# A graph-attention layer whose softmax picks one neighbour: another order of work after the last block of rows is read

## The chip, the cores and the metric

The kernel runs on one core of a Trainium2 chip, in float32. The metric is the device time of one execution in microseconds (us), as the median of several runs: 233.98 us for the kernel before (3 runs, 233.89 to 234.09).

## The reference

Inputs are x (4096 x 512), a dense matrix adj (4096 x 4096) that is added to the attention scores, W (512 x 2048, four heads of 512 columns) and a (four heads, 1024 numbers each). Cut to what matters:

```python
ht  = (x @ W) split into 4 heads
e   = leaky_relu(src[:, :, None] + dst[:, None, :], 0.01) + adj      # src, dst: ht times the two halves of a
att = softmax(e, axis=-1)
y   = (att @ ht).mean(over heads)
out = layernorm(x + y)                                               # over the 512 columns, eps 1e-5
```

The entries of adj go up to 1e9, while the scores are small. So in nearly every row the softmax is 1 at the largest entry of adj's row and 0 elsewhere, and y is that one row of x times the mean of the four heads of W. The kernel computes this, and also proves for each row that the largest entry leads the second by more than the scores can make up (a bound from the norms of x, W and a). Rows without that proof go through a second, general program, which is in the kernel but isn't entered on these data.

## The kernel before, in words

**Blocks.** The 4096 rows are 32 blocks of 128, numbered 0 to 31. A loop over t reads block t of adj (2 MB) by SyncE's DMA queue, five blocks ahead. VectorE takes the maxima of segments of each row (L215; for block 31 of the whole row, L208) and finds the segment with the largest; GpSimd gathers that segment (`lead`) and, when VectorE has found the column in it (L273, L281), the row of x that it names (`y`, L253 or L258). TensorE transposes y (`turn`, L287, into `tp`), ScalarE copies the result to SBUF (`yt`, L289), and TensorE multiplies it by the mean of W's heads (`products`, L306, four matmuls to a block, into a PSUM tile `o`). Most blocks get x by one more matmul with the identity (`residual`, L299). Blocks 22 to 27 don't: ScalarE puts their products by in SBUF (`put_by`, L354), since x for them lands late, in a buffer that adj has left, and GpSimd adds it (`add_x`, L358). Block 28 gets its x from VectorE (`add_sums`, L361), and so does block 30; block 31 is computed in two halves of 256 columns, each in its own PSUM tile.

**Normalising.** There are two ways. ScalarE sums a block and its squares (`stats`, L367 and L369), GpSimd makes shift and factor of the sums (`late_factors`, L385 to L387, the root by a power), and ScalarE scales (`finish`, L392). Or VectorE takes mean and variance (`moments`, L412 and L416), ScalarE the root (L418), VectorE the reciprocal (`factor`, L421, and with shift=True also minus mean times factor, L423), and then VectorE (`normalise`, L428) or ScalarE (`finish`) scales.

**The proof.** ScalarE sums the squares of each block of x (`row_norm`, L351) into a column of xx and takes the root of all (L623). `bound` finds the largest of them over all rows: VectorE's maximum along the columns (xm, L499), TensorE's transposition (px, L501), VectorE's maximum of that (xg, L503), TensorE's spreading over 128 partitions (px again, L506), ScalarE's bound from it (lead_by, L508). `test` (L514 to L521) compares the leads with it on VectorE, `count` adds up the rows that pass with a matmul (L527), `report` writes what is missing (any_bad, L531), which each engine reads before it decides on the general program.

**What sets the order.** Nothing reorders the instructions: the program is written out by hand, each engine takes its own instructions in the order in which the code names them, and waits on semaphores for the others. After the loop stands a long list of calls, the drain, in which blocks 28 to 31 are finished, blocks 22 to 27 get their x and are normalised, and the proof is completed. NB is 32, Q 4, LATE 28, BEHIND 24 and PUT 22. Stores go through SyncE's queue, also in order: 0 to 19 early, then 20 to 23, 28 and 29, 24 and 25, 26 and 27, 30, 31.

Of the kernel before, what the change touches and what calls it, by code (L numbers as in the profile page):

```python
# [13 lines left out]
AF = mybir.ActivationFunctionType  # L14
# [59 lines left out]
def leading_rows(ctx, tc, x, adj, W, a, out, ident, leads, any_bad):  # L74
# [14 lines left out]
    Q = 4  # L89
# [202 lines left out]
    def turn(ib):  # L292
        yt_of[ib] = turned_rows(y_t.pop(ib))

    def residual(ib):
        start = ib not in o_ps
        if start:
            o_ps[ib] = psum.tile([P, D], F32, name="o")
        nc.tensor.matmul(o_ps[ib], ident, hold[:, ib, :], start=start, stop=False)  # L299
# [48 lines left out]
    def row_norm(ib):  # L348
        sq = rows.tile([P, D], F32, name="sq")
        x_of = late_x[0][:, ib - PUT, :] if PUT <= ib < LATE else hold[:, ib, :]  # L350
        nc.scalar.activation(sq, x_of, AF.Square, accum_out=xx[:, ib : ib + 1])  # L351
# [8 lines left out]
    def add_sums(ib, out):  # L360
        nc.vector.tensor_add(out, o_ps[ib], hold[:, ib, :])  # L361
        o_ps[ib] = out
# [21 lines left out]
    def late_factors(i):  # L384
        nc.gpsimd.tensor_scalar(sd[:, i], sd[:, i], 1.0 / D, EPS, op0=OP.mult, op1=OP.add)  # L385
        nc.gpsimd.tensor_tensor(sd[:, i], sd[:, i], power[:, : i.stop - i.start], op=OP.pow)
        nc.gpsimd.tensor_mul(nm[:, i], nm[:, i], sd[:, i])  # L387

    def finish(ib):
        i = slice(ib, ib + 1)  # L390
        o = hold[:, ib, :] if ib < BEHIND else o_ps.pop(ib)
        nc.scalar.activation(hold[:, ib, :], o, AF.Identity, bias=nm[:, i], scale=sd[:, i])  # L392

    def residual_in_halves(ib):
        o_ps[ib] = [psum.tile([P, D // 2], F32, name="o") for _ in range(2)]
        for k, o in enumerate(o_ps[ib]):
            nc.tensor.matmul(o, ident, hold[:, ib, ts(k, D // 2)], start=True, stop=False)
# [10 lines left out]
    def moments(ib):  # L408

        if ib < NB - 1:  # L410
            st = small.tile([P, nc.vector.BN_STATS_DIM], F32, name="st", bufs=2)
            nc.vector.bn_stats(st, o_ps[ib])  # L412
        else:
            st = halves_st
        mv = mean_var[ib] = small.tile([P, nc.vector.BN_AGGR_DIM], F32, name="mv", bufs=3)
        nc.vector.bn_aggr(mv, st)  # L416
        r = rt[ib] = sd[:, ib : ib + 1]
        nc.scalar.activation(r, mv[:, 1:2], AF.Sqrt, bias=eps)  # L418
# [8 lines left out]
    def normalise(ib, o, columns=slice(0, D)):  # L427
        nc.vector.tensor_scalar(  # L428
            hold[:, ib, columns], o, mean_var[ib][:, 0:1], rt[ib], op0=OP.subtract, op1=OP.mult
        )  # L430
# [64 lines left out]
    def bound(part):  # L495

        if part == 0:
            xm = once.tile([P, 1], F32, name="xm")
            nc.vector.tensor_reduce(xm, xx, axis=AX.X, op=OP.max)  # L499
            px = of_bound[0] = psum.tile([1, P], F32, name="px", bufs=1)  # L500
            nc.tensor.transpose(px, xm, ident)  # L501
        elif part == 1:
            nc.vector.tensor_reduce(xg, of_bound[0], axis=AX.X, op=OP.max)  # L503
        elif part == 2:
            pb = of_bound[2] = psum.tile([P, 1], F32, name="px", bufs=1)
            nc.tensor.matmul(pb, ones[0:1, :], xg, start=True, stop=True)  # L506
        else:
            nc.scalar.activation(lead_by, of_bound[2], AF.Identity, bias=floor, scale=vn)  # L508
# [39 lines left out]
    for t in range(NB):  # L548
# [39 lines left out]
            row_norm(LATE)  # L588
            row_norm(LATE + 1)
        if t == NB - 1:  # L590
            for late in (PUT, PUT + 1):
                row_norm(late)
            residual(LATE + 1)
        if ib >= 0:
            if ib in TABLED:
                spread(ib)
# [20 lines left out]
        for done in FINISHED.get(t, ()):  # L617
            finish(done)

    for ib in (BEHIND, LATE + 2, BEHIND + 2):  # L620
        row_norm(ib)
        row_norm(ib + 1)
    nc.scalar.activation(xx, xx, AF.Sqrt, scale=1.05 ** 2)  # L623
    for ib in range(0, BEHIND - Q, Q):
        store(nc.sync, ib, Q)
    add_x(PUT)
# [5 lines left out]
        add_x(ib)  # L632
    products(LATE, KB - 1, KB)
    turn(NB - 3)
    residual_in_halves(NB - 1)
    products(NB - 3, 0, 2)
    moments(PUT)
    moments(PUT + 1)
    bound(0)
    stats(BEHIND)  # L640
    add_sums(LATE, o_ps[LATE])
    products(NB - 3, 2, KB - 1)
    moments(LATE)
    factor(PUT)
    normalise(PUT, o_ps.pop(PUT))
    bound(1)
    bound(2)
    bound(3)
    factor(PUT + 1)
    normalise(PUT + 1, o_ps.pop(PUT + 1))  # L650
    store(nc.sync, BEHIND - Q, Q)
    factor(LATE)
    normalise(LATE, o_ps.pop(LATE))
    for ib in range(BEHIND, NB - 1):
        find_inner(ib)
    turn(NB - 2)
    products(NB - 3, KB - 1, KB)
    stats(BEHIND + 1)
    late_factors(slice(BEHIND, BEHIND + 2))
    moments(NB - 3)  # L660
    test()
    products(NB - 2, 0, KB - 1)
    pg = count()
    stats(BEHIND + 2)
    late_factors(slice(BEHIND + 2, BEHIND + 3))
    factor(NB - 3)
    normalise(NB - 3, o_ps.pop(NB - 3))
    report(pg)
    finish(BEHIND)
    turn(NB - 1)  # L670
    products(NB - 2, KB - 1, KB)
    moments(LATE - 1)
    factor(LATE - 1, shift=True)
    finish(BEHIND + 1)
    products_of_half(NB - 1, 0)
    products_of_half(NB - 1, 1)
    add_sums(NB - 2, hold[:, NB - 2, :])
    moments(NB - 2)
    finish(BEHIND + 2)
    stats_of_half(NB - 1, 0)  # L680
    factor(NB - 2)
    normalise(NB - 2, o_ps.pop(NB - 2))
# [194 lines left out]
```

## Time and profile before

| | |
|---|---|
| median of 3 runs | 233.98 us |
| the profiled execution | 233.94 us |
| its span, first to last instruction | 232.4 us |
| busy: TensorE, VectorE, ScalarE, GpSimd | 84%, 84%, 64%, 49% |
| mean DMA rate over the span | 413 GB/s |
| last block of adj in use by VectorE | from 203.18 us |
| drain, from there to the last instruction of compute (229.02 us) | 25.8 us |

In the profile PE is TensorE, PEld its weight loads, DVE VectorE, ACT ScalarE, POOL GpSimd and SP SyncE. A row of a timeline has the start in us from the span's start, the length in us, engine, line and operation, what it writes and reads with shapes, and how many instructions are merged (x4); in brackets stands for how long the engine was idle just before, and what ended that. A float32 matmul is two records. Rows overlap by up to 0.1 us, since an engine begins an instruction before the last one's end is recorded. The chain of waits goes back from the last instruction, at each step to what released it.

### The profile page before, as it was taken

What the parts mean: (1) busy time and instruction counts of PE and PEld (TensorE: products, weight loads), DVE (VectorE), ACT (ScalarE), POOL (GpSimd) and SP (SyncE); (2) the same over time, 40 slices, a digit from 0 to 9 for tenths busy, and PEclk for the clock granted to TensorE, in tenths of its full rate; (3) what the DMA queues carried; (4) which work ended last, traced back from release to release, by engine and by line L of the source; (5) the groups of instructions that cost most, each with busy time, mean ns of one, the idle gap of its engine ahead of it and who ended that gap; (6) DMA issues with size and microseconds to landing.
All of it is one profiled execution on the core that took longest, in us unless ns stands there. A gap on an engine that the chain in (4) does not pass through costs nothing.

```text
span 232.4 us, 2519 instructions
## 1 busy us (share of the span) xinstructions
PE 196.0 (84%) x610; PEld 94.6 (41%) x610; DVE 194.1 (84%) x301; ACT 149.3 (64%) x371; POOL 113.5 (49%) x254
## 2 busy tenths in 40 slices
PE   0068988879069999999999899999999999999890
PEld 0023443333034445444444444454544445444360
DVE  0447299849999999999699959989999999889982
ACT  3004113597145988899988778778888746959572
POOL 4020414523555556555635665556556675468330
PEclk9999999999758999999999999999999999999999
DMA  6999999999999999999999999999999999999984
GB/s 223 434 429 430 429 430 425 433 433 422 423 437 425 414 438 427 424 427 426 428 432 424 425 429 429 425 426 430 426 430 414 420 424 421 421 420 430 426 330 193
DMA packets 12227, 96.04 MB, mean 413 GB/s; under 512 B 2020, under 2 KB 2468, under 8 KB 6064
## 3 DMA queue, kind: packets, MB, share of 16 engines
q1 hardware_dynamic: 8640, 88.08, 89.7%
q0 software_dynamic: 3552, 7.73, 8.5%
q8 instruction: 6, 0.10, 0.2%
q14 instruction: 13, 0.11, 0.1%
q10 hardware_dynamic: 16, 0.02, 0.0%
HBM read 88.51 MB, written 8.39 MB: 417 GB/s over the span
## 4 chain that ended last, share of the span: by engine, by line
DMA 38%; PE 29%; DVE 25%; ACT 3%; issue 2%; POOL 1%; SPq 0%; DVEq 0%; POOLq 0%
DMA adj_t<-in_adj_dram 29%; DVE seg L215 19%; PE o L306 18%; DMA hold<-in_L_gnn_W_dram 5%; DMA y<-in_x_dram,col 4%; PE o L346 3%; PE tp L287 3%; PE o L299 2%; DVE at L227 2%; DVE top L225 2%; PE o L401 2%; ACT sq L351 1%; DVE hold L428 1%; DVE within L273 1%; ACT off L336 0%
## 5 line engine op out<-in xcount | busy, mean ns | idle before, releaser
L215 DVE TENSOR_REDUCE seg<-adj_t 128x128 f32<-128x2048 f32 (+4 forms) x54 | 138.8, 2588 | 25.5 <-DMA adj_t<-in_adj_dram 25.4
L306 PE MATMUL o<-w_sum,yt 128*128 128x512 f32 x248 | 113.5, 597 | 1.1 <-ACT yt L289 1.1
L306 PEld LDWEIGHTS o<-w_sum,yt 128*128 128x128 f32 x248 | 46.7, 192 | 49.7 <-issue 42.3
L233 POOL DMA_INDIRECT lead<-in_adj_dram,row x31 | 32.5, 1048 | 14.5 <-POOL row L229 14.5
L229 POOL TENSOR_TENSOR row<-at,first 128x1 uint32<-128x1 uint32 x31 | 5.8, 188 | 60.6 <-DVE at L227 45.9
L258 POOL DMA_INDIRECT y<-in_x_dram,col x27 | 29.1, 1078 | 12.1 <-POOL col L275 6.8
L287 PE MATMUL tp<-ident,y 128*128 128x128 f32 x128 | 22.8, 302 | 10.0 <-DMA y<-in_x_dram,col 10.0
L452 PE MATMUL o<-hold,ident 128*128 128x512 f32 x32 | 15.7, 649 | 15.0 <-DMA hold<-in_L_gnn_W_dram 15.0
L287 PEld LDWEIGHTS tp<-ident,y 128*128 128x128 f32 x128 | 18.3, 210 | 20.7 <-issue 14.0
L289 ACT COPY yt<-tp 128x512 f32<-128x512 f32 x33 | 18.9, 572 | 11.5 <-PE tp L287 11.5
L336 ACT ACTIVATE off<-px,minus 128x128 f32<-128x128 f32 x27 | 9.9, 366 | 24.3 <-PE px L334 22.7
L299 PE MATMUL o<-hold,ident 128*128 128x512 f32 x46 | 24.4, 614 | 0.0
L346 PE MATMUL o<-z,pick 128*128 128x512 bf16 x81 | 22.6, 389 | 1.7 <-ACT pick L338 1.7
L392 ACT ACTIVATE hold<-hold,nm,sd 128x512 f32<-128x512 f32 x26 | 20.5, 802 | 0.0
L453 ACT ACTIVATE w_sum<-o 128x512 f32<-128x512 f32 x4 | 2.4, 597 | 22.9 <-PE o L452 22.9
L375 ACT ACTIVATE sq<-hold,nm 128x512 f32<-128x512 f32 x22 | 15.9, 722 | 0.7
L248 ACT COPY y<-zero 128x512 f32<-128x512 f32 x27 | 16.3, 603 | 0.0
L351 ACT ACTIVATE sq<-hold 128x512 f32<-128x512 f32 x26 | 16.2, 624 | 0.0
L452 PEld LDWEIGHTS o<-hold,ident 128*128 128x128 f32 x32 | 6.5, 211 | 23.3 <-issue 21.4
L346 PEld LDWEIGHTS <-pick 128*128 128x128 bf16 x81 | 7.6, 100 | 20.5 <-issue 9.3
L373 ACT ACTIVATE hold<-o 128x512 f32<-128x512 f32 x22 | 13.1, 597 | 0.7
L225 DVE MAX8 top<-seg 128x8 f32<-128x256 f32 (+2 forms) x31 | 11.3, 366 | 1.1
(117 smaller groups left out, 197.9 us busy)
## 6 DMA issues: line engine op xcount, KB each, us to landing
adj_t<-in_adj_dram SPq DMA_DIRECT2D x28, 2048.0 KB, 30.6
adj_t<-in_adj_dram SPq DMA_DIRECT2D x8, 1024.0 KB, 28.2
out_dram<-hold SPq DMA_DIRECT2D x5, 1024.0 KB, 17.2
hold<-in_L_gnn_W_dram SPq DMA_DIRECT2D x2, 2048.0 KB, 12.3
hold<-in_x_dram SPq DMA_DIRECT2D x3, 1024.0 KB, 32.6
hold<-in_x_dram SPq DMA_DIRECT2D x1, 1792.0 KB
hold<-in_x_dram SPq DMA_DIRECT2D x3, 512.0 KB, 24.1
out_dram<-hold SPq DMA_DIRECT2D x3, 512.0 KB, 2.8
```

Source lines behind the costliest of these rows:

```text
L215: nc.vector.tensor_reduce(seg_of[ib][:, ts(k, N // e // n)], adj_t[ib][:, ts(k, N // n)].rearrange("p (s e) -> p s e", e=e), axis=AX.X, op ...
L233: nc.gpsimd.indirect_dma_start(out=lead, out_offset=None, in_=adj_segs[e], in_offset=bass.IndirectOffsetOnAxis(ap=row[:, :1], axis=0),)
L248: nc.scalar.copy(y, zero.to_broadcast([P, D]))
L258: nc.gpsimd.indirect_dma_start(out=y_t[ib], out_offset=None, in_=x, in_offset=bass.IndirectOffsetOnAxis(ap=col[:, :1], axis=0), bounds_che ...
L287: nc.tensor.transpose(tp[:, kb, :], y[:, ds(kb, P, KB)], ident)
L289: nc.scalar.copy(yt, tp)
L299: nc.tensor.matmul(o_ps[ib], ident, hold[:, ib, :], start=start, stop=False)
L306: nc.tensor.matmul(o_ps[ib], yt_of[ib][:, kb, :], w_sum[:, kb, :], start=(start and kb == 0), stop=(kb == KB - 1),)
L346: nc.tensor.matmul(o_ps[ib], pick, z[k], start=(start and k == 0), stop=False)
L351: nc.scalar.activation(sq, x_of, AF.Square, accum_out=xx[:, ib : ib + 1])
L392: nc.scalar.activation(hold[:, ib, :], o, AF.Identity, bias=nm[:, i], scale=sd[:, i])
L452: nc.tensor.matmul(o, ident, hold[:, w_at + kb * H + h, :], start=(h == 0), stop=(h == H - 1))
```

## The change

All of it lies in the last pass of the loop and in the drain. The matmul that added x to block 29 is gone, and VectorE adds it after the products (L361, into PSUM). Blocks 22 and 23, which VectorE normalised, are scaled by ScalarE; VectorE computes their shift for it. The sum of squares of block 23 moves from the loop into the drain, and those of 26 and 27, with the root of all behind them, move behind the transposition of block 29. VectorE's maximum xm stands behind block 28's addition. The read of the largest norm (xg) stands ahead of VectorE's normalisations, its spreading behind the transposes of block 30. `test` stands ahead of block 29's addition and statistics. The sums of block 26 stand behind block 31's copy on ScalarE, and its factor comes from a root on ScalarE, a reciprocal and a product on VectorE (`last_factors`) in place of GpSimd's three instructions.

```diff
+    def last_factors(ib):
+        i = slice(ib, ib + 1)
+        nc.vector.reciprocal(sd[:, i], sd[:, i])
+        nc.vector.tensor_mul(nm[:, i], nm[:, i], sd[:, i])
@@ in the loop
         if t == NB - 1:
-            for late in (PUT, PUT + 1):
-                row_norm(late)
-            residual(LATE + 1)
+            row_norm(PUT)
@@ the drain
-    for ib in (BEHIND, LATE + 2, BEHIND + 2):
+    for ib in (PUT + 1, BEHIND, BEHIND + 1, NB - 2, NB - 1):
         row_norm(ib)
-        row_norm(ib + 1)
-    nc.scalar.activation(xx, xx, AF.Sqrt, scale=1.05 ** 2)
...
     turn(NB - 3)
+    row_norm(BEHIND + 2)
+    row_norm(BEHIND + 3)
+    nc.scalar.activation(xx, xx, AF.Sqrt, scale=1.05 ** 2)
     residual_in_halves(NB - 1)
     products(NB - 3, 0, 2)
     moments(PUT)
     moments(PUT + 1)
+    add_sums(LATE, o_ps[LATE])
     bound(0)
     stats(BEHIND)
-    add_sums(LATE, o_ps[LATE])
+    moments(LATE)
+    factor(PUT, shift=True)
+    factor(PUT + 1, shift=True)
     products(NB - 3, 2, KB - 1)
-    moments(LATE)
-    factor(PUT)
-    normalise(PUT, o_ps.pop(PUT))
     bound(1)
-    bound(2)
-    bound(3)
-    factor(PUT + 1)
-    normalise(PUT + 1, o_ps.pop(PUT + 1))
-    store(nc.sync, BEHIND - Q, Q)
     factor(LATE)
     normalise(LATE, o_ps.pop(LATE))
+    turn(NB - 2)
+    bound(2)
+    products(NB - 3, KB - 1, KB)
+    bound(3)
+    finish(PUT)
+    finish(PUT + 1)
+    store(nc.sync, BEHIND - Q, Q)
     for ib in range(BEHIND, NB - 1):
         find_inner(ib)
-    turn(NB - 2)
-    products(NB - 3, KB - 1, KB)
+    test()
     stats(BEHIND + 1)
     late_factors(slice(BEHIND, BEHIND + 2))
+    add_sums(NB - 3, o_ps[NB - 3])
     moments(NB - 3)
-    test()
     products(NB - 2, 0, KB - 1)
     pg = count()
+    report(pg)
+    turn(NB - 1)
+    products(NB - 2, KB - 1, KB)
     stats(BEHIND + 2)
-    late_factors(slice(BEHIND + 2, BEHIND + 3))
+    root(slice(BEHIND + 2, BEHIND + 3))
+    finish(BEHIND)
     factor(NB - 3)
     normalise(NB - 3, o_ps.pop(NB - 3))
-    report(pg)
-    finish(BEHIND)
-    turn(NB - 1)
-    products(NB - 2, KB - 1, KB)
     moments(LATE - 1)
-    factor(LATE - 1, shift=True)
     finish(BEHIND + 1)
     products_of_half(NB - 1, 0)
     products_of_half(NB - 1, 1)
+    last_factors(BEHIND + 2)
+    factor(LATE - 1, shift=True)
     add_sums(NB - 2, hold[:, NB - 2, :])
+    finish(BEHIND + 2)
     moments(NB - 2)
-    finish(BEHIND + 2)
```

The lines behind L388 move by five, so L428 before is L433 of the changed kernel. Three places of the engines' queues show what the diff does. VectorE around the read of the largest norm, before (from the addition of block 28; L428 are the normalisations of 22, 23 and 28):

```order
L361 TENSOR_TENSOR o<-o,hold 128x512
L412 BN_STATS st<-o 128x6
L416 BN_AGGR mv<-st 128x2
L421 RECIPROCAL sd<-sd 128x1
L428 TENSOR_SCALAR hold<-hold,mv,sd 128x512
L503 TENSOR_REDUCE xg<-px 1x1
L421 RECIPROCAL sd<-sd 128x1
L428 TENSOR_SCALAR hold<-hold,mv,sd 128x512
L421 RECIPROCAL sd<-sd 128x1
L428 TENSOR_SCALAR hold<-o,mv,sd 128x512
```

and in the changed kernel (L428 are now the shifts of 22 and 23, L433 the normalisation of 28):

```order
L361 TENSOR_TENSOR o<-o,hold 128x512
L504 TENSOR_REDUCE xm<-xx 128x1
L417 BN_STATS st<-o 128x6
L421 BN_AGGR mv<-st 128x2
L426 RECIPROCAL sd<-sd 128x1
L428 SCALAR_TENSOR_TENSOR nm<-mv,sd 128x1
L426 RECIPROCAL sd<-sd 128x1
L428 SCALAR_TENSOR_TENSOR nm<-mv,sd 128x1
L508 TENSOR_REDUCE xg<-px 1x1
L426 RECIPROCAL sd<-sd 128x1
L433 TENSOR_SCALAR hold<-o,mv,sd 128x512
```

The normalisations of 22 and 23 are gone from between the statistics of 28 and xg; a reciprocal and a shift of one column for each of the two blocks stand there.

TensorE in the same place, before (the two products are block 29's, then the transposition of xm, 29's third product, the spreading of xg, the transposes of block 30):

```order
L306 MATMUL o<-w_sum,yt 128x512 x2
L501 MATMUL px<-ident,xm 1x128
L306 MATMUL o<-w_sum,yt 128x512
L506 MATMUL px<-xg,ones 128x1
L287 MATMUL tp<-ident,y 128x128 x4
L306 MATMUL o<-w_sum,yt 128x512 x4
L527 MATMUL px<-leading,ones 1x1
```

and in the changed kernel:

```order
L306 MATMUL o<-w_sum,yt 128x512 x2
L506 MATMUL px<-ident,xm 1x128
L306 MATMUL o<-w_sum,yt 128x512
L287 MATMUL tp<-ident,y 128x128 x4
L511 MATMUL px<-xg,ones 128x1
L306 MATMUL o<-w_sum,yt 128x512 x4
L532 MATMUL px<-leading,ones 1x1
```

The transposes of block 30 now stand ahead of the matmul that spreads xg.

ScalarE towards the end, before (from block 25's sums; L418 are the roots of 29, 27, 30 and 31, L289 the copy of block 31, L392 the scaling of 24 to 27):

```order
L367 ACTIVATE sq,nm<-hold 128x512
L369 ACTIVATE sq,sd<-hold,nm 128x512
L418 ACTIVATE sd<-mv,eps 128x1
L367 ACTIVATE sq,nm<-hold 128x512
L369 ACTIVATE sq,sd<-hold,nm 128x512
L392 ACTIVATE hold<-hold,nm,sd 128x512
L289 COPY yt<-tp 128x512
L418 ACTIVATE sd<-mv,eps 128x1
L392 ACTIVATE hold<-hold,nm,sd 128x512
L418 ACTIVATE sd<-mv,eps 128x1
L392 ACTIVATE hold<-hold,nm,sd 128x512 x2
```

and in the changed kernel (L378 is the root of 26, L397 the scaling):

```order
L367 ACTIVATE sq,nm<-hold 128x512
L369 ACTIVATE sq,sd<-hold,nm 128x512
L423 ACTIVATE sd<-mv,eps 128x1
L289 COPY yt<-tp 128x512
L367 ACTIVATE sq,nm<-hold 128x512
L369 ACTIVATE sq,sd<-hold,nm 128x512
L378 ACTIVATE sd<-sd,eps 128x1
L397 ACTIVATE hold<-hold,nm,sd 128x512
L423 ACTIVATE sd<-mv,eps 128x1
L397 ACTIVATE hold<-hold,nm,sd 128x512 x2
L423 ACTIVATE sd<-mv,eps 128x1
```

Block 26's sums and the scaling of 24 have moved from ahead of block 31's copy to behind it, a root has come in, and the root of block 27 stands behind all of them.

## The prediction

> **What bounds the kernel now.** I read the span first (232.4 us for 233.94 us of the profiled execution, so 1.54 us lie around it), then the chain of waits from its end, then each engine's timeline from 204 us on. The main loop over the 32 blocks is untouched but for one matmul and one norm in its last pass, so only the last 28 us count. The chain, in order of time (start, length, what):
>
> ```profile
> 214.65 2.27 DVE hold L428
> ...
> 217.17 0.38 PE px L506 x2
> 217.55 0.68 PE tp L287 x4
> 218.23 3.52 PE o L306 x8
> 221.75 0.12 PE px L527 x2
> 221.87 0.68 PE tp L287 x4
> 222.55 0.86 PE o L306 x2
> 223.41 3.60 PE o L401 x16
> 227.03 0.44 DVE halves_st L435
> ...
> 228.46 0.56 ACT hold L441
> ```
>
> From 217.17 to 227.01 TensorE is the bound, without a gap; ahead of that it waits for xg, the largest norm. VectorE's timeline shows what xg (L503) stands behind, the normalisation of block 22 (the first L428):
>
> ```profile
> 212.93 0.69 DVE L361 TENSOR_TENSOR o<-o,hold 128x512 f32<-128x512 f32 x1
> 214.48 0.13 DVE L421 RECIPROCAL sd<-sd 128x1 f32<-128x1 f32 x1
> 214.65 2.27 DVE L428 TENSOR_SCALAR hold<-hold,mv,sd 128x512 f32<-128x512 f32 x1
> 216.85 0.27 DVE L503 TENSOR_REDUCE xg<-px 1x1 f32<-1x128 f32 x1
> 217.22 0.55 DVE L428 TENSOR_SCALAR hold<-hold,mv,sd 128x512 f32<-128x512 f32 x1
> 217.88 0.81 DVE L428 TENSOR_SCALAR hold<-o,mv,sd 128x512 f32<-128x512 f32 x1
> 220.08 0.18 DVE L416 BATCH_NORM_AGGREGATE mv<-st 128x2 f32<-128x6 f32 x1
> 220.82 0.19 DVE L521 SCALAR_TENSOR_TENSOR leads<-leads,size 128x32 f32<-128x32 f32 x1
> 223.45 0.17 DVE L421 RECIPROCAL sd<-sd 128x1 f32<-128x1 f32 x1 [0.58 <-ACT sd L418]
> 223.65 0.16 DVE L423 SCALAR_TENSOR_TENSOR nm<-mv,sd 128x1 f32<-128x1 f32 x1
> 223.73 0.69 DVE L361 TENSOR_TENSOR hold<-o,hold 128x512 f32<-128x512 f32 x1
> 225.93 0.55 DVE L428 TENSOR_SCALAR hold<-hold,mv,sd 128x512 f32<-128x512 f32 x1
> 227.03 0.43 DVE L435 BATCH_NORM_STATS2 halves_st<-o 128x6 f32<-128x256 f32 x1 [0.56 <-PE o L401]
> ```
>
> The same instruction takes 0.55 us for block 23 and 2.27 us for block 22. What differs is GpSimd, which at that moment runs its last three additions of x:
>
> ```profile
> 212.92 3.71 POOL L358 TENSOR_TENSOR hold<-hold,adj_t 128x512 f32<-128x512 f32 x3
> 220.72 0.74 POOL L386 TENSOR_TENSOR sd<-sd,power 128x2 f32<-128x2 f32 x1
> ```
>
> They end at 216.63; block 22's normalisation, if it needs its usual 0.55 us, started at 216.92 - 0.55 = 216.37, and was held 1.72 us, past the end of the second addition (212.92 + 2 x 1.24 = 215.40). So VectorE can be shut out for as long as GpSimd's additions follow each other. Not every instruction is: the reciprocal at 214.48 (one column in SBUF) and the addition at 212.93 (one operand in PSUM) ran at full pace beside them.
>
> **The change, part by part.** TensorE and ScalarE ahead of the norm:
>
> ```profile
> 205.88 1.02 PE L299 MATMUL o<-hold,ident 128*128 128x512 f32 x2
> 211.58 0.63 PE L287 MATMUL tp<-ident,y 128*128 128x128 f32 x4
> 213.32 1.98 PE L306 MATMUL o<-w_sum,yt 128*128 128x512 f32 x4 [0.24 <-ACT yt L289]
> 215.14 0.27 PE L501 MATMUL px<-ident,xm 128*1 128x128 f32 x1
> 217.48 0.75 PE L287 MATMUL tp<-ident,y 128*128 128x128 f32 x4
> 218.07 3.68 PE L306 MATMUL o<-w_sum,yt 128*128 128x512 f32 x8
> 208.75 0.63 ACT L351 ACTIVATE sq<-adj_t 128x512 f32<-128x512 f32 x1
> 212.70 0.57 ACT L289 COPY yt<-tp 128x512 f32<-128x512 f32 x1
> 220.50 0.61 ACT L367 ACTIVATE sq<-hold 128x512 f32<-128x512 f32 x1
> 221.86 0.19 ACT L369 ACTIVATION_READ_ACCUMULATOR sq<-hold,nm 128x1 f32 x1
> 221.95 0.80 ACT L392 ACTIVATE hold<-hold,nm,sd 128x512 f32<-128x512 f32 x1
> 222.66 0.56 ACT L289 COPY yt<-tp 128x512 f32<-128x512 f32 x1
> 223.12 0.29 ACT L418 ACTIVATE sd<-mv,eps 128x1 f32<-128x1 f32 x1
> ```
>
> (1) The matmul that added x of 29 goes (0.86 us in the stream, as 222.55 shows for two records). ScalarE ran six row norms from 208.75 to block 29's copy at 212.70, with a short root behind them: 0.62 us each. Now five stand there. ScalarE would be at the copy by about 211.1, and its transposes, 0.86 us sooner too, end at 212.21 - 0.86 = 211.35, so it starts near 211.4, and TensorE reaches the transposition of xm at about 213.8 instead of 215.14. The two norms and the root now follow the copy (0.46 + 1.24 + 0.4), so xm slides from 212.83 to about 213.5, still ahead of TensorE. VectorE's reciprocal of 22 comes at about 214.4 (214.48 before).
>
> (2) VectorE no longer normalises 22 and 23; it does a shift for each (the form of 223.65, 0.16 us), and xg behind them. So the first shift is due at about 214.55, while GpSimd adds until 216.63. This instruction is nowhere in the trace beside such an addition. Its hold lies between 0 (as the reciprocal) and 1.8 us (as block 22's normalisation, to 216.37); it can't be a gain. Which row is nearer? From SBUF the 512 columns take 0.55 us, from PSUM 0.81 us: the held form fetches SBUF faster, hence by more than one stream, while the rows that pass fetch one operand from SBUF. The shift has two operands there (mean and factor). I take the full hold. Against it speaks L521: two operands in SBUF, 0.19 us, inside GpSimd's 0.74 us power at 220.72; but that power has two columns, not 512, and may have read them by then.
>
> The Trainium skill, "SBUF — State Buffer", section "Who interferes with whom", says that a VectorE instruction with two SBUF inputs contends with a GpSimd instruction that reads SBUF, and that the winner keeps the shared ports for its whole length. By that rule the shifts wait, and the time is the 235.0 below; L521 should then have waited for the power's end too, and did not, and by that row there is no hold and the time is 233.2.
>
> (3) With the hold: first shift 216.37, the reciprocal of 23 and its shift, xg at 216.73 (216.85 before, 0.12 sooner). The transposes of block 30 stand ahead of xg's matmul now, in the time in which TensorE waits: block 30's 0.59 us (217.48 to 29's last product at 218.07) leaves the path. Block 31's copy started 0.11 us after its transposes' end (221.87 + 0.68), behind the scaling of 24, and 0.04 us is enough: 0.07 us. It starts at 222.66 - 0.12 - 0.59 - 0.07 = 221.88, and TensorE ends some 0.74 us sooner, near 226.25.
>
> (4) But what follows that copy is longer. Before, 26's two sums (220.50 to 221.86 + 0.19 = 222.05) and the scaling of 24 lay ahead of it; now they stand behind it, with a root for 26, and 27's root behind them all: 0.46 (222.66 to 223.12) + 1.55 + 0.03 + 0.20 (a root, 0.29, whose successor starts 0.09 us ahead of its end, as 222.66 does after 221.95 + 0.80) + 0.71 (scaling of 24) + 0.33 (root of 27, to VectorE) = 3.28 us, so 27's reciprocal starts at 225.16. Before it started 0.79 us after the copy, at 223.45. VectorE takes its queue in order, and behind that reciprocal stand 30's addition, statistics and normalisation, then the second half of 31. From the reciprocal to the end of 30's normalisation it needs 226.48 - 223.45 = 3.03 us of the same instructions; the next starts 0.08 us ahead of that end, at 228.11. Before, it waited 0.56 us for TensorE and began at 227.03; now it waits for VectorE alone.
>
> (5) The rest is as before (227.03 to 229.02, and the store). **Sum**: 228.11 - 227.03 = +1.08 us on the profiled execution's 233.94, so 235.0 us; the median of the runs, 233.98, lies 0.04 above it.
>
> Costed at nothing: 29's addition (0.72 us with its wait) and the test ahead of it. From xg to 29's variance VectorE needed 220.26 - 216.85 = 3.41 us; 23's part of it goes (217.22 to 217.88 is 0.66), the test (0.75 us, from 220.26 to 221.01) and the addition come: 4.2 us, so 29's root starts near 221.0 and lies ahead of block 31's copy (221.88) with 0.6 us to spare. Without that cover it would be on the path with what exceeds it. Scaling 22 and 23 on ScalarE (2 x 0.71 us) fills its wait for 29's variance; if ScalarE had no such wait, they would be 1.4 us on the path. 26's two factors (0.17 and 0.16 us) run while VectorE waits for 27's root. The store of 20 to 23 leaves later by about those two scalings, long ahead of the last store, which alone sets the end.
>
> **The rivals.** *No hold*: the shifts run at 214.55, xg at 214.93, 1.80 us sooner. All behind it moves as much, since the steps of (3) and (4) hang on xg one to one; xg's matmul finds the transposes just done. -0.72 us, 233.2 us. For it: the reciprocal and L521. Against it: 22's 2.27 us. The change gains while the hold is under 0.72 us. *A short hold*: the shifts slip in when the addition in flight ends (215.40, less the same 0.26 us): hold 0.6 us, -0.1 us, 233.8 us. Against it: 22's normalisation did not get in there. *TensorE stays the bound*: if ScalarE's queue after block 31's copy is shorter than I add up, only (3) counts, -0.74 us, 233.2 us with the hold. The order of ScalarE's rows speaks against it.
>
> **How the numbers follow.** Full hold 0.48, no hold 0.35, short hold 0.12, TensorE still the bound 0.05. 0.2% (0.47 us) is about what a measurement of this kernel can tell from no change. Full hold is slower nearly always (0.45 to 0.03); no hold and TensorE's case give 0.72 us and fall short of the bound in a fifth of their cases (0.32 to 0.08); a short hold is mostly within it, at times slower. Together: faster 0.33, same 0.18, slower 0.49. The likeliest time is 235.0 us; its own range is 234.5 to 235.4 (26's and 27's roots and the length of the hold, some 0.4 us either way). Since the case without a hold has more than 2 in 10, the range that holds 8 in 10 goes down to it: 233.1 to 235.3.
>
> **What would show it.** Right: a shift (L428 there) of about 1.8 us that ends with GpSimd's third addition near 216.5; xg near 216.7; TensorE's last product near 226.2; the second half's statistics begin behind VectorE, near 228.1. Shifts of 0.16 us at 214.6 make step (2) wrong; the statistics waiting for TensorE again make step (4) wrong. A wait for block 31's gather ahead of its transposes would be neither, and would make all of this wrong.

## The result, and the profile after

| | before | changed |
|---|---|---|
| median of 5 runs, side by side | 234.07 us (233.89 to 234.15) | 235.35 us (235.08 to 235.75) |
| ratio, 95% interval | | 1.0057 [1.0042, 1.0071] |
| profiled execution, its span | 233.94, 232.4 us | 235.75, 234.1 us |
| largest norm read (xg) | 216.85 | 217.04 |
| copy of block 31 | 222.66 | 222.21 |
| TensorE's last product ends | 226.99 | 226.57 |
| reciprocal of 27 | 223.45 | 225.51 |
| statistics of 31's second half | 227.03 | 228.45 |
| last arithmetic ends | 229.02 | 230.44 |

The change makes the kernel 1.28 us slower; by the interval, 0.98 to 1.66 us. Forecast were +1.08 us and 235.0 us: the sign and the main mechanism held, the time lies 0.35 above the forecast and just above the range's top, 235.3. The rows below are of the longest of the changed kernel's five executions, 0.40 us above their median, while the profiled execution of the kernel before lies 0.13 below its own. One run among the experiments, of the kernel with VectorE's scalings, took 270.27 us at a granted TensorE clock of 0.767 (0.966 to 0.985 in all others) and stands in no median or range below.

VectorE's timeline of the changed kernel (L428 are shifts now, L426 reciprocals, L440 the statistics of 31's halves):

```profile
206.95 4.42 DVE L281 FIND_INDEX8 col<-top,adj_t 128x8 uint32<-128x4096 f32 x1
...
214.12 0.19 DVE L504 TENSOR_REDUCE xm<-xx 128x1 f32<-128x32 f32 x1 [0.53 <-ACT xx L638]
215.05 0.13 DVE L426 RECIPROCAL sd<-sd 128x1 f32<-128x1 f32 x1
215.21 1.65 DVE L428 SCALAR_TENSOR_TENSOR nm<-mv,sd 128x1 f32<-128x1 f32 x1
216.97 0.16 DVE L428 SCALAR_TENSOR_TENSOR nm<-mv,sd 128x1 f32<-128x1 f32 x1
217.04 0.27 DVE L508 TENSOR_REDUCE xg<-px 1x1 f32<-1x128 f32 x1
...
225.51 0.16 DVE L426 RECIPROCAL sd<-sd 128x1 f32<-128x1 f32 x1 [0.53 <-ACT sd L423]
225.79 0.69 DVE L361 TENSOR_TENSOR hold<-o,hold 128x512 f32<-128x512 f32 x1
228.45 0.43 DVE L440 BATCH_NORM_STATS2 halves_st<-o 128x6 f32<-128x256 f32 x1
```

The shift of block 22, one column, takes 1.65 us; that of 23, the same instruction, 0.16 us. GpSimd, TensorE and ScalarE of the same kernel:

```profile
213.12 3.71 POOL L358 TENSOR_TENSOR hold<-hold,adj_t 128x512 f32<-128x512 f32 x3
...
217.37 0.38 PE L511 MATMUL px<-xg,ones 1*128 1x1 f32 x2 [1.30 <-DVE xg L508]
222.87 3.70 PE L406 MATMUL o<-w_sum,yt 128*128 128x256 f32 x16
...
212.01 0.58 ACT L289 COPY yt<-tp 128x512 f32<-128x512 f32 x1 [0.60 <-PE tp L287]
222.21 0.58 ACT L289 COPY yt<-tp 128x512 f32<-128x512 f32 x1 [0.42 <-PE tp L287]
224.30 0.29 ACT L378 ACTIVATE sd<-sd,eps 128x1 f32<-128x1 f32 x1
225.20 0.28 ACT L423 ACTIVATE sd<-mv,eps 128x1 f32<-128x1 f32 x1
227.66 0.80 ACT L397 ACTIVATE hold<-hold,nm,sd 128x512 f32<-128x512 f32 x1
229.88 0.56 ACT L446 ACTIVATE hold<-o,nm,sd 128x256 f32<-128x256 f32 x1 [0.42 <-DVE nm L428]
```

GpSimd's third addition ends at 216.83, the held shift at 216.86. TensorE waits 1.30 us for xg. Behind block 31's copy, 27's root comes only at 225.20, and the second half's statistics, which before waited 0.56 us for TensorE, show no wait: TensorE had been done for 1.9 us. The scaling of 27 (L397 at 227.66) ends at 228.46. The chain of waits of the changed kernel, in order of time:

```profile
215.21 1.65 DVE nm L428
217.42 0.81 DVE hold L433
...
222.86 2.94 DMA out_dram<-hold
225.80 0.69 DVE hold L361
```

TensorE, which carried it from 217.17 to 227.01, is gone from it; the held shift is in it. One piece has to be read with care: a store is named ahead of block 30's addition, but VectorE's timeline shows no idle time there. What VectorE did wait for was 27's root (the 0.53 us at 225.51), and the addition stands behind that in its queue.

### The profile page after: what moved, and what is told of

It is laid out like the page before. It is cut to its first block, busy times and chain, and to the rows that moved or that the text cites. A ratio compares the mean times of both kernels' runs of the same rounds, so it can differ in the third digit from the quotient of the medians.

```text
span 234.1 us, 2518 instructions
## 1 busy us (share of the span) xinstructions
PE 195.4 (83%) x608; PEld 94.4 (40%) x608; DVE 194.1 (83%) x304; ACT 151.5 (65%) x374; POOL 112.5 (48%) x251
## 4 chain that ended last, share of the span: by engine, by line
DMA 40%; DVE 28%; PE 26%; ACT 2%; issue 2%; POOL 1%; SPq 0%; DVEq 0%; POOLq 0%
DMA adj_t<-in_adj_dram 29%; DVE seg L215 19%; PE o L306 18%; DMA hold<-in_L_gnn_W_dram 5%; DMA y<-in_x_dram,col 4%; PE o L346 3%; PE tp L287 2%; PE o L299 2%; DVE at L227 2%; DVE top L225 2%; DMA out_dram<-hold 1%; DVE hold L433 1%; DVE st L417 1%; DVE nm L428 1%; DVE inner L267 1%
## 5 line engine op out<-in xcount | busy, mean ns | idle before, releaser
L289 ACT COPY yt<-tp 128x512 f32<-128x512 f32 x33 | 19.0, 575 | 13.0 <-PE tp L287 12.8
L397 ACT ACTIVATE hold<-hold,nm,sd 128x512 f32<-128x512 f32 x28 | 22.0, 802 | 0.0
```

The source lines that it names most:

```text
L289: nc.scalar.copy(yt, tp)
```

## The experiments

The theory after the result: two things cost time. GpSimd's reading of SBUF holds a VectorE instruction with two operands there, and the queue behind block 31's copy became longer than what TensorE needs. The rivals: the hold is something else (VectorE busy or waiting for data), or only one of the two halves of the change costs anything.

### The hold

*One operand.* The shifts of 22 and 23 with one tensor operand in SBUF; the factor goes in as a scalar for each partition:

```diff
-        if shift:
+        if shift and ib < BEHIND:
+            nc.vector.tensor_scalar(
+                nm[:, ib : ib + 1], mean_var[ib][:, 0:1], rt[ib], -1.0, op0=OP.mult, op1=OP.mult
+            )
+        elif shift:
```

> The changed kernel, with the shifts of 22 and 23 written as mean times factor times -1 with the factor as a scalar, so that one tensor operand instead of two is read from SBUF; nothing else differs. Theory (GpSimd's additions hold an instruction with two operands in SBUF): the shift takes about 0.16 us again, right behind its reciprocal, GpSimd's additions still running; xg and the end come some 1.45 us sooner than in the changed kernel, 233.9 us, since the shift there was due at 215.21 and ended at 216.86. Rival (VectorE waits for something else at that place, such as ScalarE or a semaphore): the shift takes 1.65 us as before, 235.3 us. Rival (any small instruction with all operands in SBUF is held): the same, 235.3 us.

Measured: 233.98 us (233.36 to 234.50, 11 runs), 0.9987 [0.9975, 0.9998] of the kernel before. GpSimd and VectorE of that kernel, in their timelines:

```profile
213.42 3.71 POOL L358 TENSOR_TENSOR hold<-hold,adj_t 128x512 f32<-128x512 f32 x3
...
215.15 0.22 DVE L428 TENSOR_SCALAR nm<-mv,sd 128x1 f32<-128x1 f32 x1
215.47 0.21 DVE L428 TENSOR_SCALAR nm<-mv,sd 128x1 f32<-128x1 f32 x1
215.60 0.27 DVE L512 TENSOR_REDUCE xg<-px 1x1 f32<-1x128 f32 x1
```

Same numbers computed, same moment, the additions running to 217.13: no hold, and xg comes 1.44 us sooner than in the changed kernel.

*No additions* of x to blocks 25 to 27 by GpSimd; these blocks then lack it.

```diff
-    for ib in range(BEHIND + 1, LATE):
-        add_x(ib)
```

> The changed kernel without GpSimd's additions of x to blocks 25, 26 and 27 (these blocks lack their x; the shifts keep their two operands). Theory (the additions are what holds the shift): the shift takes 0.16 us, xg some 1.45 us sooner, about 233.9 us. Rival (something other than GpSimd's additions holds it): shift 1.65 us, 235.3 us.

Measured: 233.99 us, one execution. The shift as the change has it, with nothing of GpSimd beside it:

```profile
215.32 0.16 DVE L428 SCALAR_TENSOR_TENSOR nm<-mv,sd 128x1 f32<-128x1 f32 x1
```

*GpSimd busy, but only writing.*

```diff
-        add_x(ib)
+        nc.gpsimd.memset(late_x[0][:, 6:8, :], 0.0)
```

> The changed kernel in which GpSimd, in place of adding x to blocks 25, 26 and 27, writes zeros three times over 1024 unused columns of the same buffer (those blocks lack their x). The writes read nothing. Theory (what is shared is GpSimd's reading of SBUF, as the Trainium skill, "SBUF — State Buffer", section "Who interferes with whom", has it for two operands): the shift of 22 takes 0.16 us beside a write, and the time is that without the additions, 234.0 us. Rival (any use of SBUF by GpSimd holds the shift): it is held to the end of the writes.

Measured: 233.73 us, one execution. The timeline:

```profile
213.25 2.98 POOL L633 MEMSET adj_t<- 128x1024 f32 x3
...
214.78 0.16 DVE L428 SCALAR_TENSOR_TENSOR nm<-mv,sd 128x1 f32<-128x1 f32 x1
```

The shift runs at full pace inside the memsets. So for this shift the hold needs GpSimd instructions that read SBUF and two tensor operands there; a GpSimd that is busy writing is not enough. Two tensor operands are not the only form that is held, though: block 22's normalisation in the kernel before has one, of 512 columns, and took 2.27 us for its usual 0.55. What sets it apart from the one-operand shift, its width or something else, no run here tells.

### The two halves of the change

*Only the last part* (26's sums behind block 31's copy, its factor by ScalarE's root and VectorE), put into the kernel before:

```diff
     stats(BEHIND + 2)
-    late_factors(slice(BEHIND + 2, BEHIND + 3))
+    root(slice(BEHIND + 2, BEHIND + 3))
```

(with the order from `report` to the end, and `last_factors`, as the change has them).

> The kernel before with only the last part of the change: the sums of 26 and the scaling of 24 behind block 31's copy, the root of 26 on ScalarE and its factors on VectorE. Nothing else of the change, so xg and the normalisation of 22 are as before. Theory (the end is set by ScalarE's queue behind that copy, through 27's root, and VectorE's queue behind it): 27's reciprocal comes 3.3 us behind the copy instead of 0.8, the second half's statistics start near 228.8 instead of 227.0, and the time is 1.7 us above the kernel before, 235.7 us. Rival (TensorE's last product sets the end in both): 234.0 us, as before, or 0.1 less.

Measured: 235.67 us (235.58 to 235.78), 1.0064 [1.0049, 1.0080]. ScalarE and VectorE:

```profile
222.65 0.58 ACT L289 COPY yt<-tp 128x512 f32<-128x512 f32 x1 [1.99 <-PE tp L287]
225.95 0.16 DVE L426 RECIPROCAL sd<-sd 128x1 f32<-128x1 f32 x1 [0.53 <-ACT sd L423]
228.88 0.42 DVE L440 BATCH_NORM_STATS2 halves_st<-o 128x6 f32<-128x256 f32 x1
```

The copy comes when it came before (222.66), and 27's reciprocal 3.30 us behind it; the prediction had added that up to 3.28. ScalarE had waited 1.99 us ahead of the copy, time in which 26's sums used to be.

*Only the first part*: the changed kernel with the old order from `stats(BEHIND + 2)` on.

> The changed kernel with the last part as it was before: the sums of 26, its factors on GpSimd and the scaling of 24 ahead of block 31's copy. The shifts keep two operands and are held to GpSimd's last addition. Theory: block 31's copy now waits for ScalarE, which sums 26 and scales 24 first, so it starts near 223.6 where the changed kernel has 222.2; TensorE ends 0.9 us later than before, and with it the kernel: 234.9 us. Rival (with the old last part, the gain of the transposes ahead of xg's matmul comes through): 233.3 us.

Measured: 235.19 us (234.87 to 235.27), 1.0036 [1.0023, 1.0049]; 0.3 above what was expected. VectorE, ScalarE and TensorE:

```profile
215.12 1.81 DVE L428 SCALAR_TENSOR_TENSOR nm<-mv,sd 128x1 f32<-128x1 f32 x1
223.94 0.56 ACT L289 COPY yt<-tp 128x512 f32<-128x512 f32 x1
224.55 3.72 PE L406 MATMUL o<-w_sum,yt 128*128 128x256 f32 x16 [1.44 <-ACT yt L289]
228.31 0.43 DVE L440 BATCH_NORM_STATS2 halves_st<-o 128x6 f32<-128x256 f32 x1 [0.56 <-PE o L406]
```

xg is held as before, but ScalarE now also scales 22 and 23 (1.51 us), so with 26's sums still ahead of it block 31's copy slips from 222.66 to 223.94 and TensorE waits 1.44 us for it. Each half alone is slower, the first by way of TensorE, the second past it. Together they cost less than the sum: with 26's sums behind the copy there is room for the two scalings ahead of it, and the copy starts at 222.21.

### A shorter queue, and what then ends the kernel

*27's root first*: the hold stays; behind the copy ScalarE scales 24 and takes 27's root at once, then 26's sums and root, and scales 25 to 27 at the end.

```diff
     turn(NB - 1)
     products(NB - 2, KB - 1, KB)
-    stats(BEHIND + 2)
-    root(slice(BEHIND + 2, BEHIND + 3))
     finish(BEHIND)
     factor(NB - 3)
     normalise(NB - 3, o_ps.pop(NB - 3))
     moments(LATE - 1)
-    finish(BEHIND + 1)
+    stats(BEHIND + 2)
+    root(slice(BEHIND + 2, BEHIND + 3))
...
-    last_factors(BEHIND + 2)
     factor(LATE - 1, shift=True)
     add_sums(NB - 2, hold[:, NB - 2, :])
+    moments(NB - 2)
+    finish(BEHIND + 1)
+    last_factors(BEHIND + 2)
     finish(BEHIND + 2)
-    moments(NB - 2)
```

> The changed kernel (the shifts still held) with another order behind block 31's copy: ScalarE scales 24, then takes 27's root, then 26's sums and root, 30's root, and scales 25, 26, 27; VectorE makes 26's factors behind 30's statistics. Theory (the end hangs on 27's root and VectorE's queue behind it): 27's reciprocal comes near 224.0 instead of 225.5, the second half's statistics near 227.2 instead of 228.45, then ScalarE's scaling of 27 is in the way of the last root by 0.4 us; 0.9 us sooner than the changed kernel, 234.4 us. Rival (something else ends the kernel, such as the stores): 235.3 us.

Measured: 235.48 us (235.36 to 235.89), 1.0058 [1.0043, 1.0074]: a miss. ScalarE's scalings and the last arithmetic, then the stretches of 1 us (the last two numbers are the share of the DMA engines' time and GB/s):

```profile
225.79 2.21 ACT L397 ACTIVATE hold<-hold,nm,sd 128x512 f32<-128x512 f32 x3
228.61 0.56 ACT L446 ACTIVATE hold<-o,nm,sd 128x256 f32<-128x256 f32 x1 [0.42 <-DVE nm L428]
```

```profile
226.00:227.00 1.00, 0.20 (x1) 0.00 (x0) 0.96 (x4) 1.00 (x2) 0.00 (x0) 1.00 0.06 16
227.00:228.00 1.00, 0.00 (x0) 0.00 (x0) 0.33 (x2) 1.00 (x3) 0.00 (x0) 1.00 0.59 233
228.00:229.00 1.00, 0.00 (x0) 0.00 (x0) 0.75 (x3) 0.58 (x2) 0.00 (x0) 0.95 0.84 344
229.00:230.00 1.00, 0.00 (x0) 0.00 (x0) 0.03 (x1) 0.17 (x1) 0.00 (x0) 0.50 1.04 426
230.00:231.00 1.00, 0.00 (x0) 0.00 (x0) 0.00 (x0) 0.00 (x0) 0.00 (x0) 0.50 0.99 375
```

The arithmetic ends at 229.17, 1.27 us sooner than in the changed kernel. Of that 0.38 us was there before the drain (GpSimd's last additions start at 212.74, 213.12 there), and 0.9 us is what was reckoned. Nothing is gained: the span ends at 233.8, 4.63 us behind it (3.66 in the changed kernel). The stores of 24 to 27 all leave late, the DMA engines stand idle first and are full afterwards. So the last store alone does not set the end.

*The same with one-operand shifts*:

> Both mends: the shifts with one tensor operand, and the order of the run before this one behind block 31's copy. Theory: the copy as in the kernel with the one-operand shift (221.1), 27's reciprocal near 222.9 instead of 224.4, the second half's statistics near 226.0 instead of 227.3, the end 0.9 us sooner than with the one-operand shift alone: 233.1 us, 0.5% below the kernel before. Rival (the two gains don't add, since TensorE's or the gather's wait takes over): 233.9 us.

Measured: 234.55 us (234.33 to 234.79), 1.0015 [1.0006, 1.0024]: again a miss, with the arithmetic done at 228.15 and 4.65 us to the end of the span (232.8).

*That kernel with 27 scaled at the very end*, behind 31's root:

```diff
     normalise(NB - 2, o_ps.pop(NB - 2))
-    finish(LATE - 1)
     stats_of_half(NB - 1, 1)
     moments(NB - 1)
+    finish(LATE - 1)
```

> As the run before this one, and ScalarE scales 27 behind the root of 31 instead of ahead of it. Theory: the last root no longer waits 0.4 us for that scaling, but the last scaling does in part: 232.9 us. Rival (the store of 26 and 27 now goes out beside the last one and holds it): 233.3 us or more.

Measured: 234.99 us (234.64 to 235.28), 1.0031 [1.0020, 1.0041]. The arithmetic ends at 228.18 as before that edit, 27 is scaled at 227.72 (226.98), and the span ends at 233.6 (232.8): 0.74 us later scaled, 0.8 us later done. Of this 0.23 us was there ahead of the edited place (block 31's copy at 220.89 for 220.66); the medians differ by 0.44 us. The end hangs on the store of 26 and 27. Whether by that store, or by everything still queued, two kernels tell that leave a store out, each made from the kernel with one-operand shifts and 27's root first (234.55 us):

```diff
-    for ib, n in ((LATE, 2), (BEHIND, 2), (BEHIND + 2, 2), (NB - 2, 1)):
+    for ib, n in ((LATE, 2), (BEHIND + 2, 2), (NB - 2, 1)):
```

> The kernel with one-operand shifts and 27's root first, without the store of blocks 24 and 25 (512 KB; those rows of the output are not written, all the arithmetic is done). In that kernel (234.55 us, span 232.8) the arithmetic ends at 228.15, the DMA queues stand nearly idle to 226.5 and then move the stores of 24 to 27, 30 and 31, 1.5 MB, without a gap at about 0.4 MB per us until 230.7. Theory (what sets the end is the amount still to be stored when 27 is scaled, at the DMA rate): without 512 KB the store of 26 and 27 starts at once when 27 is scaled (226.98), its data and those of 30 and 31 (1 MB, 2.6 us) are through by about 230.3, held up then by 31's own late start rather than by the queue: span about 232.0, time about 233.8 us, 0.6 to 0.9 sooner. Rival (a fixed time from 27's scaling, or from the last arithmetic, to the end, whatever else is stored): the same 234.5 us.

```diff
-    for ib, n in ((LATE, 2), (BEHIND, 2), (BEHIND + 2, 2), (NB - 2, 1)):
+    for ib, n in ((LATE, 2), (BEHIND, 2), (NB - 2, 1)):
```

> The same kernel without the store of blocks 26 and 27 instead (512 KB; those rows are not written, all the arithmetic is done). Theory: the store of 24 and 25 is through by about 228.0, ahead of those of 30 and 31 (256 KB each, released at 226.2 and 228.15); only 31's own store follows the last arithmetic, so the end comes 3.1 to 3.4 us behind 228.15, at 231.3 to 231.6: time 233.0 to 233.3 us, 1.2 to 1.5 sooner. Rival (the last arithmetic or a fixed length of the end decides): 234.5 us; if only the store of 24 and 25 mattered, as much as without that.

Measured: 234.48 us (234.31 to 234.98) without the store of 24 and 25, 1.0009 [1.0000, 1.0019] of the kernel before; 233.08 us (232.87 to 233.39) without that of 26 and 27, 0.9947 [0.9930, 0.9963]; 234.55 and 1.0015 with both. The stretches of the first of the two:

```profile
227.00:228.00 1.00, 0.00 (x0) 0.00 (x0) 0.28 (x3) 0.66 (x2) 0.00 (x0) 1.00 0.00 0
228.00:229.00 1.00, 0.00 (x0) 0.00 (x0) 0.51 (x2) 0.56 (x1) 0.00 (x0) 1.00 0.71 291
229.00:230.00 1.00, 0.00 (x0) 0.00 (x0) 0.00 (x0) 0.00 (x0) 0.00 (x0) 0.98 0.99 395
230.00:231.00 1.00, 0.00 (x0) 0.00 (x0) 0.00 (x0) 0.00 (x0) 0.00 (x0) 0.50 0.97 361
```

Here 27 is scaled at 227.48, and the 1 MB of 26, 27, 30 and 31 moves from about 228.2 to 231.0, as long as it does behind the store of 24 and 25. My theory was wrong in one half, then: what is queued ahead costs about 0.1 us, not the 0.6 to 0.9 expected. What costs is the store of 26 and 27 with what stands behind it (233.08 is within the 233.0 to 233.3 expected). In the profiles of all kernels that have this store it begins 0.7 to 0.9 us behind the scaling of the later of 26 and 27, and where it and the two stores behind it, 1 MB, move without a gap they need some 2.7 us.

What follows is longer in some kernels than in others, and finer stretches show a part of the reason: when the bulk is through, single packets still trickle. In the kernel before, then in the one with one-operand shifts and 27's root first:

```profile
230.60:230.80 0.20, 0.00 (x0) 0.00 (x0) 0.00 (x0) 0.00 (x0) 0.00 (x0) 1.00 0.33 113
...
230.40:231.40 1.00, 0.00 (x0) 0.00 (x0) 0.00 (x0) 0.00 (x0) 0.00 (x0) 0.50 0.12 35
```

They last 0.2 us in the first and 1.0 us in the second; with 27 scaled last and without the store of 24 and 25 it is 1.0 us too. Behind the last packet it is another 1.6 and 1.4 us to the end of the span, and 1.1 to 1.8 us in the fourteen profiles of this study. Why the packets trickle longer in some kernels stays open. The Trainium skill, "DMA: Bandwidth & Descriptors", section "Anatomy of one DMA — SWDGE (gpsimd) path", puts about 2 us of fixed cost on a transfer, most of it the wait for the last write's receipt; that is written of another path than that of these stores, but the size agrees: here about 0.8 us ahead of the data and 1.1 to 1.8 us behind the last packet. How much of it is a receipt, no run here shows.

### Towards a faster kernel

*24 and 25 scaled by VectorE*, on top of the one-operand shifts; ScalarE scales 27 sooner too, ahead of 30's root (`finish_on_vector` is one `tensor_scalar` with factor and shift):

```diff
-    finish(BEHIND)
...
-    finish(BEHIND + 1)
+    finish_on_vector(BEHIND)
+    finish_on_vector(BEHIND + 1)
...
     finish(BEHIND + 2)
+    finish(LATE - 1)
     moments(NB - 2)
...
-    finish(LATE - 1)
```

> The changed kernel with the one-operand shifts (so without the hold), and with the scalings of 24 and 25 by VectorE (one tensor_scalar each, 0.55 us for 128x512 from SBUF, by the rows of block 23 before) ahead of 27's reciprocal's turn, while VectorE waits for ScalarE. ScalarE's queue behind block 31's copy is then 26's sums, 26's root, 27's root: 0.7 us shorter than in the kernel with one-operand shifts alone. Theory (the end is the later of two: the second half's statistics, which follow 27's reciprocal, plus about 5.3 us; and the scaling of 27, which releases the store of 26 and 27, plus 5.1 to 5.9 us): 27's reciprocal near 223.8 (224.37 there), the second half's statistics near 226.7 (227.31), the last arithmetic ends near 228.7 (229.29), 27 is scaled by about 225.5 to 226.8, and since 24 and 25 are stored about 1.5 us sooner, their store no longer lies on top of that of 26 and 27: about 233.2 to 233.4 us, 0.6 to 0.8 under the kernel with one-operand shifts alone. Rival (the stores take the same time from a fixed moment, however early the arithmetic ends): 233.9 to 234.2 us, with 4.0 us or more between the last arithmetic and the end.

Measured: 233.88 us median (233.15 to 234.27), 0.9986 [0.9976, 0.9997]. The arithmetic ends at 228.38, sooner than expected, 27 is scaled at 225.11, and still the profiled execution needs 4.2 us to the end of its span: the rival's case, for which no run here gives the cause. Its times fall into two groups, two at 233.15 and 233.18 and nine from 233.75 to 234.27, and the profile is of one of the nine; what separates them no row tells.

*26's mean and variance by VectorE*, on top of the one-operand shifts; 27 is scaled ahead of 26:

```diff
-    stats(BEHIND + 2)
-    root(slice(BEHIND + 2, BEHIND + 3))
...
     moments(LATE - 1)
     finish(BEHIND + 1)
+    moments(BEHIND + 2)
...
-    last_factors(BEHIND + 2)
     factor(LATE - 1, shift=True)
     add_sums(NB - 2, hold[:, NB - 2, :])
+    finish(LATE - 1)
+    moments(NB - 2)
+    factor(BEHIND + 2, shift=True)
     finish(BEHIND + 2)
-    moments(NB - 2)
...
     normalise(NB - 2, o_ps.pop(NB - 2))
-    finish(LATE - 1)
```

> The changed kernel with the one-operand shifts, and block 26's mean and variance taken by VectorE's statistics (0.69 us) in place of ScalarE's two sums (1.55 us from the first one's start to the next instruction) and its root of sums. Behind block 31's copy ScalarE then has the scaling of 24, 27's root, the scaling of 25, 26's root, the scaling of 27. Theory: 27's reciprocal near 223.25 (224.37 with one-operand shifts alone), the second half's statistics near 226.4 (227.31), where TensorE's product, ended near 226.0, is next to bind; the last arithmetic ends near 228.4 (229.29) and the store of 26 and 27 leaves near 226.5: about 233.0 us, 0.9 to 1.0 under the kernel with one-operand shifts alone and about 0.4% under the kernel before. Rival (the stores set the end whatever the arithmetic does): 233.9 to 234.2 us.

Measured: 233.12 us median (233.07 to 233.88), 0.9958 [0.9946, 0.9971] of the kernel before: faster by 0.98 us, the best of the kernels that write every row, and as expected. ScalarE and VectorE:

```profile
220.74 0.59 ACT L289 COPY yt<-tp 128x512 f32<-128x512 f32 x1 [0.48 <-PE tp L287]
223.05 0.28 ACT L423 ACTIVATE sd<-mv,eps 128x1 f32<-128x1 f32 x1
224.98 0.81 ACT L397 ACTIVATE hold<-hold,nm,sd 128x512 f32<-128x512 f32 x1
227.26 0.56 ACT L450 ACTIVATE hold<-o,nm,sd 128x256 f32<-128x256 f32 x1 [0.42 <-DVE nm L432]
...
222.03 0.66 DVE L417 BATCH_NORM_STATS2 st<-hold 128x6 f32<-128x512 f32 x1
222.82 0.13 DVE L426 RECIPROCAL sd<-sd 128x1 f32<-128x1 f32 x1
225.84 0.42 DVE L444 BATCH_NORM_STATS2 halves_st<-o 128x6 f32<-128x256 f32 x1
```

26's statistics (0.66 us at 222.03) run while VectorE would have waited for a root. 27's reciprocal comes at 222.82, 2.1 us behind the copy instead of 3.3, and the last of blocks 24 to 27 is scaled by 225.79, ahead of the last arithmetic by 2.0 us.

All kernels side by side (us; the last three columns from the profiled execution):

| kernel | median | 26 and 27 scaled | last arithmetic | span |
|---|---|---|---|---|
| before | 234.07 | 227.10 | 229.02 | 232.4 |
| changed | 235.35 | 228.46 | 230.44 | 234.1 |
| one operand | 233.98 | 227.32 | 229.29 | 232.6 |
| 27's root first | 235.48 | 228.00 | 229.17 | 233.8 |
| both of these | 234.55 | 226.98 | 228.15 | 232.8 |
| 27 scaled last | 234.99 | 227.72 | 228.18 | 233.6 |
| 24, 25 by VectorE | 233.88 | 225.11 | 228.38 | 232.6 |
| 26 by VectorE | 233.12 | 225.79 | 227.82 | 232.3 |

The profiled execution of the last one, at 233.88 us, is the longest of its five; the spans of the other four are 231.4 to 231.6.

## Why the prediction was right or wrong

**Step (1), TensorE and ScalarE ahead of the norm: wrong in size, without effect.** Block 29's copy was to come 1.3 us sooner; it came 0.7 us sooner (212.01 against 212.70). Of the missing 0.6 us, 0.35 arose ahead of the step: TensorE's six records of products at 203.30 before stand at 203.65. The rest lies right ahead of the transposes of 29, whose first weight load comes behind a gap of 0.82 us, where 0.24 is usual:

```profile
211.22 0.56 PEld L287 LDWEIGHTS tp<-ident,y 128*128 128x128 f32 x4 [0.82 <-issue]
```

The profile names no releaser here. The step counted engines only and left out block 29's gathered rows of x, and in the kernel with VectorE's scalings, as in five others of the experiments, these are what releases the transposes; that they do so in the changed kernel too is likely, but not shown. The chain of the kernel with VectorE's scalings:

```profile
203.66 7.29 DMA y<-in_x_dram,col
211.09 0.73 PE tp L287 x4
```

They land at 210.95 there, and no shorter queue on TensorE gets past that. So the shift was due at 215.21, not 214.55, and it was luck that this did no harm: the hold swallowed the difference. It shows where there is no hold. The rival "no hold" gave -0.72 us, and the kernel with one-operand shifts, which is that case, gains 0.30 us (0.05 to 0.59) on the kernel before. Had the shifts passed, the forecast of a gain would have been some 0.4 us too good.

**Step (2), the full hold: right.** It ended 0.03 us behind GpSimd's third addition, and lasted 1.65 us for the "up to 1.8" since the shift was due later. The shift fell due inside the second addition (213.12 + 1.24 = 214.36 to 215.59) and did not get in when the third began, which rules out "a short hold". The Trainium skill, "SBUF — State Buffer", section "Who interferes with whom", has the rule that two SBUF inputs contend with a GpSimd instruction that reads SBUF but not with one that only writes it: the additions, the one-operand form and the memsets here agree, with 1.65, 0.22 and 0.16 us. By itself that rule does not account for block 22's normalisation, held with one tensor operand in SBUF. What spoke against it, the unheld L521 beside the two-column power, no run here explains.

**Step (3), block 30's transposes off the path: right, but the end of the hold was mis-sized.** xg was forecast for 216.73 and came at 217.04. Of that 0.31 us, 0.20 arose before the drain (the last search for a column starts at 206.95, 206.75 before, and GpSimd's additions end 0.20 later). 0.11 us is the hold's release: the step let the shift start 0.26 us ahead of the end of GpSimd's additions, as block 22's normalisation did if it needed its 0.55 us, and so end 0.10 us ahead of it; the shift ended 0.03 us behind it. Block 31's copy (222.21 for 221.88) and TensorE's end (226.57 for 226.25) moved with it.

**Step (4), the queue behind block 31's copy: right.** Forecast 3.28 us from the copy to 27's reciprocal, measured 3.30; then 2.95 us to the second half's statistics, measured 2.94. Without a wait for TensorE, as forecast. That these two sums were free before because ScalarE waited there, the last part alone shows: it costs 1.50 us by itself.

**Step (5), "The rest is as before", "the last store, which alone sets the end" and the sum: too small.** The sum came to 235.02 us, measured are 235.35. Of the 0.33 us, 0.13 is the base: the sum stands on one execution of 233.94, and beside the changed kernel the kernel before took 234.07. 0.20 us is the difference, +1.28 for +1.08. The one term of it that the runs show mis-sized is the hold's end in step (3), 0.11 us: with the first part alone and with 27's root first the shift too ends 0.02 and 0.03 us behind GpSimd's additions. The other 0.09 us lies inside the interval and can't be assigned. The profile can't do it, since its execution is a long one: its last arithmetic ends 1.42 us later than before, 0.20 of that from before the drain (GpSimd's last additions start anywhere from 212.74 to 213.42 us in the profiles of kernels that are the same up to there), and from there to the end of the span it takes 3.66 us for 3.38. With the last part alone, whose queue is the same, that is 3.13 us (230.87 to 234.0), and single packets trickle for 0.5 us there, for 0.8 us in the changed kernel; so the 0.28 us are not shown to belong to the change.

That the last store alone sets the end was wrong as a mechanism. The store of 26 and 27, released by the scaling of 27, decides as well, as the kernel without it shows by 1.5 us. In the changed kernel that scaling came 1.36 us later than before (228.46 against 227.10), so either account gives it much the same time; the error is small here and large in the experiments that rested on it, 27's root first above all.

**The range** failed by its top. The prediction's own range for the full hold, 234.5 to 235.4, holds the 235.35; the range of 8 in 10 was drawn down to the case without a hold and cut at 235.3. Nor did it allow for the spread of runs of one kernel, 235.08 to 235.75 for this one.

## What to carry to other kernels

A one-column instruction can cost as much as a large one: when VectorE has to get a number out while GpSimd streams from SBUF, try a form with one tensor operand there, which helped the one-column shift (a normalisation of 512 columns with one operand was held all the same), or keep GpSimd's reads away from that moment. Work that fills another engine's wait is free only in that place: the two sums of block 26 cost 1.5 us when they moved from ahead of a copy, where ScalarE then stood idle, to behind it. At the end of a kernel find which large store is released last and how much stands behind it, before the last arithmetic is made sooner; 0.9 us won there were worth nothing while that store left late.

## What the runs showed of the hardware that was not expected

VectorE's held instruction did not come in between GpSimd's successive additions in the three kernels that have the shift in its two-operand form beside them: it ended 0.03 us behind the last one in the changed kernel (1.65 us from start to end), 0.02 us behind it with the first part alone (1.81 us, 216.93 against 213.20 + 3.71) and 0.03 us behind it with 27's root first (1.49 us, 216.49 against 212.74 + 3.72). And an execution can end over 4 us behind its last arithmetic, where the kernel before needs 3.4: with 26 by VectorE the profiled one has its DMA engines almost empty from 230 us on (share 0.01, then none) and its span ends at 232.3. What is awaited there no row tells.
